# The second step of a graph layer: logits in two pairs, and one scaling moved from GpSimd to VectorE

## The chip, the cores and the metric

The kernel runs on one core of a Trainium2 chip. A core has five engines, each with its own queue of instructions, which they work off in order: TensorE (PE in the profile; its loads of the stationary operand are shown apart, as PEld), VectorE (DVE), ScalarE (ACT), GpSimd (POOL) and SyncE (SP), which here only starts transfers. They meet through semaphores. The metric is the time of one execution on the device, in microseconds; the number given is the median of several runs.

## The reference

3327 nodes with 256 features each (x), and a dense adjacency matrix (adj) in which few entries are not zero. The input is normalised and passed through a ReLU; call the result h. Then two steps run:

- `A = top_p_attention(Xa)`: for each node a query and a key of 64 numbers, `logits = q @ k.T` (3327 x 3327), a softmax over each row, of which only the largest entries that together make up 0.9 are kept; the rows are scaled to sum to one again.
- `Xf = R @ Xf` with R = adj + identity, rows scaled to sum to one, and `Xa = A @ Xa`.
- `Z = Z + Xf @ U1[n].T + Xa @ U2[n].T`.

At the end `h + Z` is normalised over the features (mean and variance), multiplied by `ln_g`, `ln_b` is added, and so is the input x.

## The kernel before, in words

The nodes are padded to 3328 and cut into NT = 26 tiles of 128 rows. For each tile and each step the kernel computes a row block e of exponentials of the logits, 128 x 3328 in fp32, finds for each row the threshold above which 0.9 of the mass lies, sets the smaller entries to zero, and multiplies what is left with the 3328 x 256 features.

All of this is a pipeline over the tiles, written out by hand. Loop i of a step works on several tiles at once, each at another stage. A loop is cut into PARTS = 7 slots. For each slot the strings in `PLAN` (and `OPEN`, `LAST` for the first and last loops of the second step) say in which order pieces of work are emitted; each letter advances one generator to its next `yield`. Since every engine works in order, and the last lines tie the order of the text as a dependency for each engine, this order is the order in each queue. The pieces of the second step, in loop i:

- w, `weights` (L580 and the lines behind): logits and exponentials of tile i + 2. Keys of even tiles stand in the lower 64 partitions of `after`, those of odd tiles in the upper 64, and so the query is held twice. Four chunks; each has two matmuls (lower and upper half, 416 columns each, L597) into one of two PSUM buffers `pl` of two banks, and an exponential on ScalarE that reads both halves (L601) with a sum. The last chunk leaves out the padded column, and a further exponential of one column (L609) makes up for it. So e has all even tiles first and then all odd ones.
- m and, in the next loop, n, `measured_twice`: estimates of the threshold of tile i + 1. It begins in `guessed`, where ScalarE adds up the partial sums in `za` to Z (L619) and goes on with small instructions (L620 to L624). Then follow three passes over e on ScalarE (L632, output `ja`), one for each of three slots, with small instructions on VectorE (L682, L683, L694, L695, L701, L702) and GpSimd (L673 to L675, L686 to L689, L703 to L707) between them.
- d and, in the next loop, c, `settle`: on VectorE the entries below the estimate (L724), the largest of each piece of 168 columns (L729) and of those again (L736, L738), sums (L743), the exact threshold, and in the first slot of the next loop the cut of e at it (L758).
- the transposes: `turn` (L804) transposes e on TensorE, four 128 x 128 blocks at a time, and ScalarE copies them to SBUF (L806). In the second step it is called at the head of each slot, before the letters; in the slot with k = 2 two groups of four are turned, and they are the first of a new tile. They need L758 of that tile to have ended.
- the sums: `sum` (L818) multiplies the transposed blocks with the features and accumulates in PSUM (`pa`), at the end of a slot. The block with number c of e belongs to feature tile `c % HALF * 2 + c // HALF`.
- s and g, `spread` and `fetching`: the product with R from gathered rows (L928 on TensorE, L1156 on VectorE; the gathers are issued by GpSimd, L920).
- f, `finish`, in four parts: the scaled sum on VectorE (L979), mean and variance on VectorE (L463, L464), the inverse deviation rstd on GpSimd (L470, L471), and in the third slot of the next loop four instructions on GpSimd: centring and scaling (L998), times gamma (L999), input plus beta (L1000), and their sum (L1001); then the row block is written out. The last tile of all does this on VectorE.

After the second step a check in the kernel proves that every threshold is exact; if it fails, a second algorithm (`search_graph_layer`) computes everything again. The first tiles of the second step have their logits computed at the end of the first one.

Of the kernel before, what the change touches and what calls it, by code (L numbers as in the profile page):

```python
# [9 lines left out]
F32 = mybir.dt.float32  # L10
# [3 lines left out]
AF = mybir.ActivationFunctionType  # L14
ALU = mybir.AluOpType
AX = mybir.AxisListType
PSUM = bass.MemoryType.PSUM

P = 128
# [3 lines left out]
NT = (N + P - 1) // P  # L23
# [301 lines left out]
HALF = NT // 2  # L325
PARTS = -(-NT // 4)
AHEAD = (2, 2)
COUNTED = [t for t in range(NT - 2) if t % 2 == 0]
HALVES = 7
FIRST = 8 * P  # L330
CUT = 4

# [12 lines left out]
def guess_graph_layer(ctx, tc, x, adj, w1t, w2t, w3t, u1t, u2t, ln_g, ln_b, out, flag):  # L347
# [10 lines left out]
    ps_l = ctx.enter_context(tc.tile_pool(name="ps_l", bufs=2, space=PSUM))  # L358
# [4 lines left out]
    V, G, S, PE = nc.vector, nc.gpsimd, nc.scalar, nc.tensor  # L363
# [10 lines left out]
    both = nodes.tile([P, 2, HALF, P], F32, tag="both", name="both")  # L374
    after = nodes.tile([P, HALF, P], F32, tag="after", name="after")
    low, high = slice(0, DA), slice(DA, P)
    keys_of = lambda step, a: after[(low, high)[a]] if step else both[(low, high)[a], a]
    query_at = lambda t: (high, low)[t % 2]
    query_of = lambda t: both[query_at(t), t % 2, t // 2, :]
    es = [nodes.tile([P, NP], F32, tag=f"e{k}", name=f"e{k}") for k in range(4)]  # L380
# [195 lines left out]
    def law_of(t):  # L576

        return lambda k: law[:, {7: 1, 8: 4}.get(k, k), t : t + 1]

    def weights(step, t, live, known=True):  # L580

        r = dict(Z=rec[:, step, 3, t : t + 1])
        qT = asked(t)
        yield
        r["ms"] = law_of(t) if known and step else early.get(t)
        lawful = law_once(step, t) if known and not step else none
        r["e"] = e = es[(2, 3, 0, 1, 4, 5)[t % 6] if step else t % 4]
        r["za"] = za = small.tile([P, CUT + 1], F32, tag="za", name="za")
        live[step, t] = r
        w = HALF * P  # L590
        wd = w // CUT
        for n in range(CUT):
            c = n * wd
            pl = ps_l.tile([P, 2, 512], F32, tag="pl", name="pl")
            for a in range(2):
                p = slice(a * DA, (a + 1) * DA)
                PE.matmul(pl[:, a, :wd], qT[p, :],  # L597
                          keys_of(step, a).rearrange("p a b -> p (a b)")[:, c : c + wd],
                          start=True, stop=True)
            if n < CUT - 1:  # L600
                S.activation(e.rearrange("p (a n) -> p a n", a=2)[:, :, c : c + wd], pl[:, :, :wd],  # L601
                             AF.Exp, accum_out=za[:, n : n + 1])
                if known and not step and n < 2:
                    r["ms"] = returned(lawful) if n else next(lawful)
                yield
            else:
                S.activation(e.rearrange("p (a n) -> p a n", a=2)[:, :, c : w - 1], pl[:, :, : wd - 1],
                             AF.Exp, accum_out=za[:, n : n + 1])
                S.activation(e[:, w - 1 : w], pl[:, 0, wd - 1 : wd], AF.Exp, accum_out=za[:, n + 1 :])  # L609
# [5 lines left out]
    def guessed(r, g, step):  # L615

        r["col"] = col = lambda k: g[:, k : k + 1]
        ms = r["ms"]
        S.activation(r["za"], r["za"], AF.Copy, accum_out=r["Z"])  # L619
        S.activation(col(0), r["Z"], AF.Ln)  # L620
        S.activation(col(2), col(0), AF.Relu, scale=-0.25, bias=ms(7))
        S.activation(col(2), col(2), AF.Exp, scale=-1.0, bias=con((6, 9)[step]))
        S.activation(col(3), col(2), AF.Square, bias=con((3, 8)[step]))
        S.activation(col(9), col(3), AF.Exp, scale=ms(3), bias=ms(8))  # L624
        return col
# [165 lines left out]
    class Sums:  # L791
# [18 lines left out]
        def sum(self, g):  # L810

            t, k = divmod(g, PARTS)
            if k == 0:
                self.pa = ps_a.tile([P, 2 * D], F32, tag="pa", name="pa")[:, :D]
            eT = self.eT.pop(g)
            for c in range(4 * k, min(4 * k + 4, NT)):
                j = c % HALF * 2 + c // HALF
                PE.matmul(self.pa, eT[:, c - 4 * k, :], self.xa[:, j, :], start=c == 0, stop=c == NT - 1)  # L818
            if k < PARTS - 1:
                return None  # L820
            if self.step:
                return t, (self.pa, self.live.pop((self.step, t))["ra"])
            n = rows_of(t)
            dst = row.tile([P, D], F32, tag="xa", name="xa", bufs=2)
            if n < P:
                V.memset(dst, 0.0)
            S.activation(dst[:n], self.pa[:n], AF.Copy, scale=self.live.pop((self.step, t))["ra"][:n])
            return t, dst
# [149 lines left out]
    def finish(t, y, pa, ra):  # L978
        V.scalar_tensor_tensor(y, pa, ra, y, ALU.mult, ALU.add)  # L979
        yield  # L980
        mv = spread_of(y)
        yield
        if t < NT - 1:
            xr = row.tile([P, D], F32, tag="xr", name="xr", bufs=1)
            nc.sync.dma_start(xr, x[t * P : (t + 1) * P])
        if t == NT - 1:
            rstd = small.tile([P, 1], F32, tag="rstd", name="rstd")
            S.activation(rstd, mv[:, 1:2], AF.Ln, bias=con(10))
            S.activation(rstd, rstd, AF.Exp, scale=-0.5)
        else:  # L990
            rstd = inverse(mv)
        yield
        if t == NT - 1:
            xr = live["x"]
            V.scalar_tensor_tensor(y, y, mv[:, 0:1], gam, ALU.subtract, ALU.mult)
            V.scalar_tensor_tensor(y, y, rstd, xr, ALU.mult, ALU.add)
        else:
            G.tensor_scalar(y, y, mv[:, 0:1], rstd, ALU.subtract, ALU.mult)  # L998
            G.tensor_tensor(y, y, gam, ALU.mult)  # L999
            G.tensor_tensor(xr, xr, bet, ALU.add)  # L1000
            G.tensor_tensor(y, y, xr, ALU.add)  # L1001
        h = rows_of(t)
        whole = h // 16 * 16
        nc.sync.dma_start(out[t * P : t * P + whole], y[:whole])
        if whole < h:
            nc.scalar.dma_start(out[t * P + whole : t * P + h], y[whole:h])
# [156 lines left out]
    def refetch(t):  # L1163
# [7 lines left out]


    PLAN = (("gmdsssaz", "gmcdsssaz", "edawwpg", "gmsdga", "gmspdea", "ohgdawwqg", "gehmgq"),
            ("llcmss", "lnms", "lwwnfd", "lcmdsssgggg", "fdswmqdf", "llmd", "lwmfdg"))

    LAST = {NT - 1: ("cfss", "cn", "nd", "sss", "fddddddsf", "f", ""), NT: ("c", "", "", "ff", "ff", "fv", "f"),
            NT + 1: ("fv", "f", "", "", "f", "f", "f")}
# [2 lines left out]
             1: ("ggmdsssbb", "gmcdgsssbb", "gedbwwbp", "bmsdg", "gmpdeg", "hgdwwqg", "hgemgqo"),  # L1180
             NT + 1: ("", "weweee", "", "", "", "", ""),
             2: ("gmdsssa", "gmcdsssga", "gedawwpg", "gmsdga", "gmspdea", "ohgdawwqg", "gehmgq")}
    OPEN = {-1: ("mxx", "mxll", "mlgg", "mgll", "mw", "mll", "mgggg"),
            0: ("cmggg", "nm", "nfd", "cmd", "fdlxmgqdf", "mwdf", "mwd"),
            1: ("cmss", "nms", "wwnfd", "cmdsssgggg", "fdsmwqdf", "mgdf", "mwdg")}
    OPEN[2] = OPEN[3] = OPEN[1]
    spacing = itertools.chain(spaced((0, 1)), *(spaced((t,)) for t in range(2, NT)))
    fetching = itertools.chain(*(refetch(t) for t in range(NT)))
# [22 lines left out]
    for step in range(2):  # L1211
        sums = Sums(step, live, xw if step else x0, AHEAD[step])

        for i in range(-1, NT + 2):
# [44 lines left out]
            for k in range(PARTS):  # L1259
# [7 lines left out]
                    prove(0)  # L1267
                g = PARTS * (i - 1) + k - LATE[step]
                summing = valid(g // PARTS)
                if step and valid((g + AHEAD[1]) // PARTS):  # L1270
                    sums.turn(g + (k == 2), min(i, NT - 1))
                for c in ({**OPEN, **LAST} if step else BEGIN).get(i, PLAN[step])[k]:
                    at = len(trace)
                    next(work[c], None)
                    if c == "g" and not step and len(trace) > at:
# [76 lines left out]
```

## Time and profile before

| what | value |
|---|---|
| median of three runs | 1305.98 us (1303.44 to 1306.17) |
| the profiled execution | 1309.6 us |
| its span, from the first to the last instruction | 1307.5 us |
| mean granted TensorE clock | 0.984 |
| busy: PE, DVE, ACT, POOL | 96%, 87%, 82%, 76% of the span |
| DMA, mean over the span | 117 GB/s |

The first step takes somewhat more than half of the span; the logits of the second one begin at 667 us, its steady part lies between some 770 and 1230 us. Busy time is the union of the instructions of an engine; matmuls overlap, and a busy PE is not PE at its peak. In the chain of waits each row names the instruction that the end waited for at that time; in a timeline the bracket says how long the engine stood idle just before and what ended it. "issue" is a wait with no cause in the profile. Times in rows are counted from the start of the span.

### The profile page before, as it was taken

The page shows a single profiled execution, that of the slowest core. Times are in us where ns is not written, and L with a number is a line of the kernel's source. Part 1 is how long each engine was busy: PE and PEld are TensorE (multiplying, and loading weights), DVE is VectorE, ACT ScalarE, POOL GpSimd, SP SyncE. Part 2 cuts the span into 40 slices and gives each one's busy share as a digit, 9 for nine tenths or more (in the row PEclk, how much of TensorE's full clock was granted, in tenths as well). Part 3 has the DMA queues.
Part 4 walks back from the last instruction along what each step waited for, and adds up shares of the span by engine and source line. Part 5 has one row for each costly group of instructions (what it writes and reads, how often), then busy time and mean ns, then how long its engine had stood idle before and what let it go on. Part 6 is the DMA issues. An engine that isn't in the chain of part 4 may idle for free.

```text
span 1307.5 us, 21855 instructions
## 1 busy us (share of the span) xinstructions
PE 1255.1 (96%) x6336; PEld 957.6 (73%) x6336; DVE 1136.7 (87%) x3437; ACT 1072.5 (82%) x2297; POOL 990.9 (76%) x1329
## 2 busy tenths in 40 slices
PE   6989899999999999999999789999999999999997
PEld 5635687777877778777777557777777777777776
DVE  6867699999999999999994579899998999999995
ACT  5375788888888888888874779999999999999961
POOL 6114788888888888888785477888888889888872
PEclk9999899999999999999999889999999999999999
DMA  8734455555455555555533231313222231322300
GB/s 289 228 124 127 146 142 150 157 147 159 138 154 153 149 158 141 145 158 151 153 88 99 76 94 51 102 55 98 72 84 81 71 98 55 98 75 79 93 22 22
DMA packets 100751, 153.11 MB, mean 117 GB/s; under 512 B 16879, under 2 KB 67182, under 8 KB 100622
## 3 DMA queue, kind: packets, MB, share of 16 engines
q1 hardware_dynamic: 83056, 108.71, 26.5%
q0 software_dynamic: 16640, 42.69, 13.0%
q8 instruction: 52, 0.85, 0.3%
q14 instruction: 77, 0.63, 0.2%
q10 hardware_dynamic: 926, 0.23, 0.1%
HBM read 120.88 MB, written 27.28 MB: 113 GB/s over the span
## 4 chain that ended last, share of the span: by engine, by line
PE 79%; DVE 7%; ACT 7%; POOL 3%; issue 2%; DMA 1%; SPq 0%; ACTq 0%; DVEq 0%; POOLq 0%
PE pa L818 38%; PE pl L597 12%; PE pt L804 10%; PE pr L928 8%; ACT ja L632 3%; PE pz L968 3%; PE pz L1044 3%; DVE cand L729 2%; PE pk L1090 1%; PE pk L490 1%; DVE x L758 1%; DVE w L724 1%; DVE cand L738 1%; DVE bb L736 1%; PE pt L479 1%
## 5 line engine op out<-in xcount | busy, mean ns | idle before, releaser
L632 ACT ACTIVATE ja<-e,g 128x3328 uint8<-128x3328 f32 x106 | 325.5, 3071 | 0.2
L818 PE MATMUL pa<-xw,eT 128*128 128x256 f32 x1352 | 322.3, 383 | 2.5 <-DVE s L979 2.5
L818 PE MATMUL pa<-x,eT 128*128 128x256 f32 x1352 | 322.6, 380 | 0.1
L818 PEld LDWEIGHTS pa<-xw,eT 128*128 128x128 f32 x1352 | 249.9, 190 | 61.8 <-issue 26.9
L818 PEld LDWEIGHTS pa<-x,eT 128*128 128x128 f32 x1352 | 243.4, 191 | 26.1 <-issue 0.4
L729 DVE MAX8 cand<-w 128x8 f32<-128x168 f32 (+1 forms) x1040 | 253.4, 319 | 0.0
L899 POOL DMA_INDIRECT ac<-in_adj,index x130 | 195.6, 1504 | 61.4 <-issue 28.0
L806 ACT COPY eT<-pt 128x512 f32<-128x512 f32 (+1 forms) x364 | 198.3, 552 | 49.5 <-PE pt L804 44.2
L920 POOL DMA_INDIRECT xg<-vx,index x130 | 191.3, 1471 | 34.7 <-issue 33.0
L920 POOL DMA_INDIRECT xg<-bx,index x130 | 157.2, 1209 | 48.5 <-issue 23.8
L804 PEld LDWEIGHTS pt<-ident,e 128*128 128x128 f32 x1144 | 138.9, 143 | 58.5 <-issue 30.5
L804 PE MATMUL pt<-ident,e 128*128 128x128 f32 x1144 | 176.5, 277 | 3.0 <-ACT mq L531 1.3
L724 DVE SCALAR_TENSOR_TENSOR w<-e,g 128x3328 f32<-128x3328 f32 x44 | 162.3, 3688 | 0.9
L928 PE MATMUL pr<-xg,ac 128*128 128x257 f32 (+1 forms) x520 | 139.3, 392 | 9.7 <-DVE s L1156 5.7
L758 DVE SCALAR_TENSOR_TENSOR e<-e,rec 128x3328 f32<-128x3328 f32 x40 | 147.2, 3680 | 0.6
L601 ACT ACTIVATE e<-pl 128x832 f32<-128x832 f32 x132 | 114.2, 867 | 37.7 <-PE pl L597 29.6
L928 PEld LDWEIGHTS pr<-xg,ac 128*128 128x128 f32 x520 | 94.1, 193 | 36.7 <-issue 14.4
L597 PE MATMUL pl<-both,qT 64*128 64x416 f32 x416 | 97.8, 548 | 7.1 <-DVE e L1050 3.6
L597 PE MATMUL pl<-after,qT 64*128 64x416 f32 x416 | 96.2, 556 | 0.1
L848 DVE TENSOR_REDUCE fm<-at 128x4 f32<-128x512 f32 (+1 forms) x133 | 84.5, 636 | 0.0
L736 DVE MAX8 bb<-cand 128x8 f32<-128x160 f32 x234 | 75.6, 323 | 4.6
L632 ACT ACTIVATE ja<-x,g 128x3328 uint8<-128x3328 f32 x24 | 73.6, 3065 | 0.0
(270 smaller groups left out, 1995.4 us busy)
## 6 DMA issues: line engine op xcount, KB each, us to landing
at<-in_adj SPq DMA_DIRECT2D x114, 256.0 KB
cx<-ac SPq DMA_DIRECT2D x26, 384.0 KB
ac<-cx SPq DMA_DIRECT2D x26, 384.0 KB
wide<-in_adj SPq DMA_DIRECT2D x8, 832.0 KB
e<-in_adj SPq DMA_DIRECT2D x6, 832.0 KB
own<-bx SPq DMA_DIRECT2D x26, 128.5 KB
x<-in_x SPq DMA_DIRECT2D x13, 256.0 KB
qT<-both SPq DMA_DIRECT2D x104, 32.0 KB
```

What stands on the lines that cost most here:

```text
L597: PE.matmul(pl[:, a, :wd], qT[p, :], keys_of(step, a).rearrange("p a b -> p (a b)")[:, c : c + wd], start=True, stop=True)
L601: S.activation(e.rearrange("p (a n) -> p a n", a=2)[:, :, c : c + wd], pl[:, :, :wd], AF.Exp, accum_out=za[:, n : n + 1])
L632: S.activation(ja, e, f, bias=guess, scale=sign, accum_out=total)
L724: V.scalar_tensor_tensor(w, e, col(16), e, ALU.is_lt, ALU.mult, accum_out=d2)
L729: V.max(cand[:, 8 * s : 8 * s + 8], w[:, s * SEG : min(NP, (s + 1) * SEG)])
L758: V.scalar_tensor_tensor(e, e, at(1), e, ALU.is_ge, ALU.mult, accum_out=ra)
L804: PE.transpose(pt[:, j, :], e[:, (j0 + j) * P : (j0 + j + 1) * P], ident)
L806: S.copy(eT[:, :w, :], pt[:, :w, :])
L818: PE.matmul(self.pa, eT[:, c - 4 * k, :], self.xa[:, j, :], start=c == 0, stop=c == NT - 1)
L899: G.indirect_dma_start(out=ac[:, k, :], out_offset=None, in_=rows, in_offset=bass.IndirectOffsetOnAxis(ap=index[:, t, k : k + 1], axis=0), ...
L920: G.indirect_dma_start(out=xg[:, k, :w], out_offset=None, in_=rows, in_offset=bass.IndirectOffsetOnAxis(ap=index[:, t, k : k + 1], axis=0))
L928: PE.matmul(pr[:, :w], ac[:, k, :], own if k == KT - 1 else xg[:, k, :w], start=k == 0, stop=k == KT - 1)
```

## The change

All parts but the tables of order concern the second step alone.

- The four chunks of logits are cut at tile pairs: 4, 3, 3 and 3 pairs, so 512, 384, 384 and 384 columns in each half (`EDGES`). Each chunk is written to e as a block of its own, even tiles and then odd ones, and `ORDER` says which feature tile a block of e belongs to. For the last chunk the lower half is written at the end of its PSUM bank, so that both halves follow each other without a gap and one exponential of 767 columns leaves out the padded column. The exponential of one column is gone.
- Z is summed on VectorE (a reduction of four numbers) in a fifth call of w, and no longer in `guessed`.
- The letters w: two in slot k = 2, one in k = 4 and one in k = 6 become two in k = 2, two in k = 4 and the fifth call in k = 6.
- A letter t places the transposes inside a slot. In k = 2 they now come behind the two w; where a slot has no t they stay at its head.
- In `finish`, L998 goes from GpSimd to VectorE for all tiles but the last.

```diff
+EDGES = (0, 4, 7, 10, 13)
+ORDER = ([2 * j + h for h in range(2) for j in range(HALF)],
+         [2 * j + h for a, b in zip(EDGES, EDGES[1:]) for h in range(2) for j in range(a, b)])
...
+    def close(qT, e, za):
+
+        keys = after.rearrange("p j r -> p (j r)")
+        for n, (j0, j1) in enumerate(zip(EDGES, EDGES[1:])):
+            c, w = j0 * P, (j1 - j0) * P
+            pl = ps_l.tile([P, 2, 512], F32, tag="pl", name="pl")
+            for p, at in ((low, pl[:, 0, 512 - w :] if n == CUT - 1 else pl[:, 0, :w]), (high, pl[:, 1, :w])):
+                PE.matmul(at, qT[p, :], keys[p, c : c + w], start=True, stop=True)
+            to = e[:, 2 * c : 2 * (c + w)]
+            if n == CUT - 1:
+                S.activation(to[:, : 2 * w - 1], pl.rearrange("p a n -> p (a n)")[:, 512 - w : 511 + w], AF.Exp,
+                             accum_out=za[:, n : n + 1])
+            else:
+                S.activation(to.rearrange("p (a n) -> p a n", a=2), pl[:, :, :w], AF.Exp, accum_out=za[:, n : n + 1])
+            yield
...
+        if step:
+            yield from close(qT, e, za)
+            V.tensor_reduce(r["Z"], za[:, :CUT], AX.X, ALU.add)
+            return
...
-        S.activation(r["za"], r["za"], AF.Copy, accum_out=r["Z"])
+        if step == 0:
+            S.activation(r["za"], r["za"], AF.Copy, accum_out=r["Z"])
...
-                j = c % HALF * 2 + c // HALF
-                PE.matmul(self.pa, eT[:, c - 4 * k, :], self.xa[:, j, :], start=c == 0, stop=c == NT - 1)
+                PE.matmul(self.pa, eT[:, c - 4 * k, :], self.xa[:, ORDER[self.step][c], :], start=c == 0, stop=c == NT - 1)
...
-            G.tensor_scalar(y, y, mv[:, 0:1], rstd, ALU.subtract, ALU.mult)
+            V.tensor_scalar(y, y, mv[:, 0:1], rstd, ALU.subtract, ALU.mult)
...
-            ("llcmss", "lnms", "lwwnfd", "lcmdsssgggg", "fdswmqdf", "llmd", "lwmfdg"))
+            ("llcmss", "lnms", "wwtlnfd", "lcmdsssgggg", "fdswwmqdf", "llmd", "lwmfdg"))
...
-    OPEN = {-1: ("mxx", "mxll", "mlgg", "mgll", "mw", "mll", "mgggg"),
+    OPEN = {-1: ("mxx", "mxll", "mlgg", "mgll", "mw", "mllw", "mgggg"),
...
-            1: ("cmss", "nms", "wwnfd", "cmdsssgggg", "fdsmwqdf", "mgdf", "mwdg")}
+            1: ("cmss", "nms", "wwtnfd", "cmdsssgggg", "fdsmwwqdf", "mgdf", "mwdg")}
...
-                if step and valid((g + AHEAD[1]) // PARTS):
-                    sums.turn(g + (k == 2), min(i, NT - 1))
-                for c in ({**OPEN, **LAST} if step else BEGIN).get(i, PLAN[step])[k]:
+                plan = ({**OPEN, **LAST} if step else BEGIN).get(i, PLAN[step])[k]
+                for c in plan if "t" in plan or not step else "t" + plan:
+                    if c == "t":
+                        if valid((g + AHEAD[1]) // PARTS):
+                            sums.turn(g + (k == 2), min(i, NT - 1))
+                        continue
```

More of the change, by code (lines that the diff above doesn't have):

```diff
@@ L376, in guess_graph_layer @@
     low, high = slice(0, DA), slice(DA, P)
-    keys_of = lambda step, a: after[(low, high)[a]] if step else both[(low, high)[a], a]
+    keys_of = lambda a: both[(low, high)[a], a]
     query_at = lambda t: (high, low)[t % 2]
@@ L597, in weights @@
                 PE.matmul(pl[:, a, :wd], qT[p, :],
-                          keys_of(step, a).rearrange("p a b -> p (a b)")[:, c : c + wd],
+                          keys_of(a).rearrange("p a b -> p (a b)")[:, c : c + wd],
                           start=True, stop=True)
@@ L602, in weights @@
                              AF.Exp, accum_out=za[:, n : n + 1])
-                if known and not step and n < 2:
+                if known and n < 2:
                     r["ms"] = returned(lawful) if n else next(lawful)
```

## The prediction

> **What bounds the kernel now.** I read the page first (busy time, then the chain that ended last), then the busy time of the middle of the second step, then the chain there in order of time, and last the instructions of one tile engine by engine.
>
> ```profile
> PE 1255.1 (96%) x6336; PEld 957.6 (73%) x6336; DVE 1136.7 (87%) x3437; ACT 1072.5 (82%) x2297; POOL 990.9 (76%) x1329
> ...
> PE 79%; DVE 7%; ACT 7%; POOL 3%; issue 2%; DMA 1%; SPq 0%; ACTq 0%; DVEq 0%; POOLq 0%
> ```
>
> ```profile
> 860.00:1230.00 370.00, 369.05 (x1895) 286.99 (x1896) 342.10 (x1002) 355.47 (x681) 322.08 (x412) 1.00 0.27 80
> ```
>
> The second row is busy time between 860 and 1230 us in the order PE, PEld, DVE, ACT, POOL, then granted clock (1.00). PE is never idle, but ACT stands at 96%, DVE at 92% and POOL at 87%: a gain on PE is soon stopped by another engine, so all four are counted. One tile on the chain (start, length, count of instructions):
>
> ```profile
> 900.79 0.44 PE pt L804 x4
> 901.23 0.90 PE pl L597 x4
> 902.12 1.92 PE pa L818 x8
> ...
> 904.49 1.73 PE pa L818 x8
> ...
> 906.65 0.90 PE pl L597 x4
> ...
> 917.48 1.60 PE pl L597 x8
> 919.08 1.49 PE pr L928 x6
> ...
> 921.44 0.44 PE pt L804 x4
> ```
>
> From turn to turn, 900.79 to 921.44, a tile takes 20.65 us, and PE sets it. The logits (pl) come in three groups, x4, x4 and x8. Twice 0.90 against 1.60 says that 0.70 us is the work of four instructions and 0.20 us a fixed cost of each group. What follows a group is dear too: 1.92 against 1.73 us for the same eight sums, and 1.49 us against 6 x 0.216 = 1.30 for the six pr. So entering and leaving the logits costs 0.20 + 0.19 = 0.39 us a group, 1.17 a tile.
>
> **The change, part by part.** *Logits on PE.* Four chunks of 416 columns become 512 + 384 + 384 + 384; that is 1664 columns in both cases, and at 0.70 us per 416 the work stays 2.80 us. I take the time as linear in the columns. Three groups become two, so PE loses one fixed cost: 20.65 - 0.39 = 20.26 us a tile. By the code the pattern stands in 23 tiles, and from the first to the last of these rows PE is the chain:
>
> ```profile
> 855.54 1.60 PE pl L597 x8
> ...
> 1228.35 1.60 PE pl L597 x8
> ```
>
> 372.81 us are 18 periods of 20.65 and 1.1 us of stall, so 19 tiles are counted in full: 19 x 0.39 = 7.4 us. Four tiles lie before 855.
>
> *Exponentials on ACT.* The same elements are read, in four instructions. The one-column exponential (L609) and the copy that sums (L619) go; what they take is from their start to the next start:
>
> ```profile
> 905.11 3.07 ACT L632 ACTIVATE ja<-e,g 128x3328 uint8<-128x3328 f32 x1
> ...
> 908.64 0.87 ACT L607 ACTIVATE e<-pl 128x830 f32<-128x830 f32 x1
> ...
> 909.48 0.17 ACT L609 ACTIVATE e<-pl 128x1 f32<-128x1 f32 x1
> ...
> 909.63 0.39 ACT L697 ACTIVATE g<-g,one 128x1 f32<-128x1 f32 x1
> ...
> 911.06 0.20 ACT L619 ACTIVATE za<-za 128x5 f32<-128x5 f32 x1
> ...
> 911.38 0.20 ACT L620 ACTIVATE g<-rec 128x1 f32<-128x1 f32 x1
> ```
>
> 0.15 + 0.32 = 0.47 us. ACT's work a tile is 355.47 / 370 x 20.65 = 19.84, after it 19.37, under 20.26.
>
> *Work put on DVE.* A sum of four numbers (L733 is the nearest row) and the centring and scaling of a 128x256 row block, which leaves POOL.
>
> ```profile
> 906.26 0.15 DVE L733 TENSOR_REDUCE rec<-cand 128x1 f32<-128x20 f32 x1
> 906.33 0.32 DVE L736 MAX8 bb<-cand 128x8 f32<-128x160 f32 x1
> ...
> 908.56 0.27 DVE L694 TENSOR_SCALAR g<-oa,g 128x1 f32<-128x1 f32 x1
> ...
> 911.55 0.58 POOL L471 TENSOR_TENSOR rstd<-rstd,half 128x1 f32<-128x1 f32 x1
> ...
> 911.64 3.69 DVE L758 SCALAR_TENSOR_TENSOR e<-e,rec 128x3328 f32<-128x3328 f32 x1
> ...
> 912.32 4.00 POOL L920 DMA_INDIRECT xg<-vx,index  x1 [0.19 <-issue]
> ...
> 915.45 3.66 DVE L724 SCALAR_TENSOR_TENSOR w<-e,g 128x3328 f32<-128x3328 f32 x1
> ...
> 916.23 1.01 PEld L804 LDWEIGHTS pt<-ident,e 128*128 128x128 f32 x8
> ...
> 916.38 2.95 POOL L673 TENSOR_SCALAR g<-g,law 128x1 f32<-128x1 f32 x1
> ...
> 920.03 1.25 POOL L998 TENSOR_SCALAR s<-s,mv,rstd 128x256 f32<-128x256 f32 x1
> ...
> 921.37 0.73 POOL L999 TENSOR_TENSOR s<-s,gam 128x256 f32<-128x256 f32 x1
> ...
> 921.48 0.48 DVE L979 SCALAR_TENSOR_TENSOR s<-pa,ra,s 128x256 f32<-128x256 f32 x1 [0.83 <-PE pa L818]
> ```
>
> ```profile
> L878 DVE TENSOR_SCALAR oh<-place,over,lists 128x128 f32<-128x128 f32 x26 | 9.0, 345 | 0.8 <-ACT lists L874 0.8
> ...
> L746 DVE TENSOR_SCALAR dr<-cum,need 128x40 f32<-128x40 f32 x26 | 6.5, 249 | 0.9
> ```
>
> An instruction that does not need the one ahead starts 0.08 us before that one ends (906.26 + 0.15 against 906.33). So the sum of four adds 0.07. For the 256 columns I extend the two TENSOR_SCALAR rows: (345 - 249) / 88 = 1.09 ns a column, 345 + 128 x 1.09 = 485 ns, 0.40 net of the overlap; below it lies the 128-column row (0.26 net), above it 0.485 + 0.15 with no overlap at all. DVE's only wait in the tile is 0.83 us at L979, with the lost overlap 0.91: its work is 19.74 us, after it 20.21 (20.07 to 20.38). Against PE's 20.26 that is a dead heat with 0.05 us left. At the upper end DVE sets 20.38, which costs 0.12 x 19 = 2.3 us; I take 0.4.
>
> *Logits ahead of the new tile's transposes.* These transposes need L758, which ends at 915.33; they begin at 916.23, 0.90 us of room. With a pair of logits ahead (512 + 384 columns: 1.5 us, and 0.2 to enter) the room becomes 2.6. It is needed: both exponentials of the second pair now stand ahead of the count (ja, 905.11 + 3.07 = 908.18) whose result L694 waits for. That count ends some 0.8 us later relative to PE (0.87 x 768 / 832); L694 at 908.56 has under 0.4 us of room, so DVE slides back by about 0.5 us, and the room at the transposes stays above 2. The next tile's sums must not start before L979 has read PSUM; ahead of them stands a pair of 1.5 us where one chunk of 0.9 stood, so a later L979 is covered too.
>
> *POOL.* Without L998 each tile has 921.37 - 920.03 = 1.34 us less. L999 now waits for DVE, where the new instruction stands between L758 and L724; POOL is then still inside L673, so it is not late. The new wait is DVE's for rstd (L471), with L724 and the whole search for the tile's threshold queued behind it. Today L471 starts 0.09 us before L758 and is done (912.13) 3.2 us before L758 ends: hidden. Uncovered, it is the slower rival.
>
> *Ends.* Before 855 the chain runs through other engines, with this POOL instruction held while DVE runs L758:
>
> ```profile
> 828.54 3.61 POOL g L705
> ```
>
> The waits between engines from 760 us on (total, times, longest) show what PE lost to late transposes, and a wait of DVE with no cause that the profile shows:
>
> ```profile
> DVE g L694 <- issue: 3.6, 6, 2.0
> ...
> PE pt L804 <- DVE x L758: 1.8, 2, 1.0
> ```
>
> The four early tiles gain 0 (the same holds recur) to 2.4 us (4 x 0.39, and 0.8, the smaller of the two late transposes, which the new room of 2.6 us would cover); I take 1.2. Of the 1.1 us of stall behind 855, which lies at the other late transpose, I take 0.5 back: its cause, DVE's 2.0 us, stays.
>
> After the last logits DVE is the chain:
>
> ```profile
> 1243.10 3.70 DVE x L758 x2
> ...
> 1267.08 3.62 DVE w L724 x2
> ```
>
> Here the moved instruction is on the path, twice: 2 x 0.40, and DVE arrives there up to 0.9 us later against PE (0.5 slid, 0.4 from the dead heat): a loss of 0 to 1.7, I take 1.2.
>
> Sum: 7.4 + 1.2 + 0.5 - 1.2 - 0.4 = 7.5 us. The profiled execution took 1309.6 us (span 1307.5), 3.6 above the median of 1305.98; its own time becomes 1302.1, and in the terms of the median 1298.5. Bounds of the terms: 7.4 - 1.7 - 2.3 = 3.4, and 7.4 + 2.4 + 1.1 = 10.9, so 1295.1 to 1302.6.
>
> **The rivals.** *DVE takes over.* If L694 keeps waiting 0.3 us in each tile for the later count, DVE needs 20.5: 19 x 0.15 + 0.5 - 1.2 = 2.2 us, 1303.8. For it: 0.05 us is no margin. Against it: DVE can slide back by two us before PE waits.
>
> *Pairs wait for ACT.* If a pair's second chunk finds its PSUM buffer unread, the fixed cost is spent again inside the pair: no gain on PE, the tail's 1.2 lost, stalls 0.5 back, about 1306.7. Against it: the pairs start 4.4 us apart at the closest (901.23 + 20.65 - 917.48), and the two exponentials of 0.87 each follow the first pair at once.
>
> *Slower: DVE waits for rstd.* If POOL starts L471 behind L758, it is held until L758 ends, as L705 was (3.61 us); L673 ended 0.2 us after L724 did, then 0.58 for L471: the new instruction stalls 0.75 us, DVE needs 20.96, PE's gain is gone and 0.31 a tile is lost: 23 x 0.31 + 1.2 = 8.3 us, 1314.3. The point: from L724's end (919.11) POOL needs 13.09 us to its next L471 (911.55 + 20.65), then 11.75; DVE comes to L758 in 13.18, then 13.18 - 0.91 + 0.07 = 12.34. So POOL must lose 0.59 us in every tile. Margin today 0.09, so the removal of L998 speaks against it; a POOL delay also sends DVE back, which restores the margin in the next tile.
>
> *Slower: the gather in flight.* L920 runs to 916.32, 0.99 us past L758's end. If a running gather kept DVE from the moved instruction, DVE would need 21.20: 23 x 0.55 + 1.2 = 13.9 us, 1319.9. The nearest rows show an instruction of this kind inside a gather at its usual length:
>
> ```profile
> 343.54 1.11 POOL L899 DMA_INDIRECT ac<-in_adj,index  x1 [0.19 <-issue]
> 343.95 0.34 DVE L878 TENSOR_SCALAR oh<-place,over,lists 128x128 f32<-128x128 f32 x1
> ```
>
> The Trainium skill has this as a rule ("SBUF — State Buffer", section "SBUF: two separate sides"): VectorE and GpSimd share a port pair; of two instructions that need it, whichever starts first holds it to its end and the other fully blocks. By that rule this rival would be the forecast; the trace agrees for POOL behind L758 (4.00 us) but not for L878 behind a gather (0.34 us).
>
> *The kernel doesn't do what it says.* The columns of e stand in another order, so another spread of large entries over the 168-column pieces is searched; if the proof fails, the second algorithm runs and the time more than doubles.
>
> **How the numbers follow.** The forecast (1298.5) 0.60, DVE takes over 0.17, pairs wait 0.08, rstd 0.10, gather 0.03, proof 0.02. About 0.2%, 2.6 us, is what a measurement can tell from no change: faster means under 1303.4, slower over 1308.6. Faster: 0.60 and half of DVE's 0.17, 0.68. Same: the other half and the pairs, 0.17. Slower 0.15. The range 1294 to 1307 holds the forecast's own and the two rivals without change; the slower 0.15 is left out, with little below.
>
> **What would show it.** Right: logits in x8 groups only, 1.7 and 1.5 us; a tile of 20.2 to 20.3 us on the chain; L979 nearly without wait; L998 on DVE in 0.4 to 0.5 us; transposes never waiting for L758. Wrong: a wait of DVE at L998 for L471 (slower), a wait at L694 in every tile (DVE takes over), PE idle between two chunks of a pair (ACT), or fixed costs that stay with each pair of chunks rather than with each group.

## The result, and the profile after

The changed kernel takes 1298.88 us (median; 1293.95 to 1301.80) against 1305.81 (1300.52 to 1308.65) for the kernel before, timed in the same rounds: a ratio of 0.9948, 95% interval 0.9935 to 0.9961, or 5.1 to 8.5 us less. 1298.5 had been forecast.

Busy time and the chain that ended last, from the page after:

```profile
PE 1237.1 (96%) x6336; PEld 950.1 (73%) x6336; DVE 1146.6 (89%) x3488; ACT 1060.7 (82%) x2193; POOL 975.3 (75%) x1304
...
PE 47%; DVE 42%; ACT 5%; issue 3%; POOL 2%; DMA 1%; SPq 0%; ACTq 0%; POOLq 0%; DVEq 0%
```

PE held 79% of the chain and DVE 7%; now they share it. The busy times of the middle of the second step after (columns as before: PE, PEld, DVE, ACT, POOL, clock) say the same:

```profile
860.00:1215.00 355.00, 353.70 (x1854) 280.19 (x1853) 341.26 (x1002) 339.11 (x600) 308.90 (x383) 1.00 0.26 80
```

DVE went from 92% to 96%, ACT stays at 96%, POOL stays at 87% of a shorter tile, and PE at over 99%.

The spans of the two profiled executions (1307.5 and 1294.2 us) differ by more than the change gives: the first step, whose work is unchanged, was some 8 us shorter in the second of them, and over the profiles of this study its end scatters by 11 us. So the second step is compared alone. Its tiles are counted by the threshold cut on DVE (L758 before, L782 after). The first and the last of the 24 cuts, before:

```profile
787.24 3.69 DVE L758 SCALAR_TENSOR_TENSOR e<-e,rec 128x3328 f32<-128x3328 f32 x1
...
1262.77 3.69 DVE L758 SCALAR_TENSOR_TENSOR e<-e,rec 128x3328 f32<-128x3328 f32 x1
```

and after:

```profile
780.47 3.69 DVE L782 SCALAR_TENSOR_TENSOR e<-e,rec 128x3328 f32<-128x3328 f32 x1
...
1247.81 3.69 DVE L782 SCALAR_TENSOR_TENSOR e<-e,rec 128x3328 f32<-128x3328 f32 x1
```

23 tiles took 475.5 us and take 467.3: 8.2 us less. Behind the last cut the end came 44.7 us later and now comes 46.3 later, 1.6 us lost; from the step's first logarithm to the first cut it was 59.9 and is 61.2, but that stretch lies anywhere between 59.9 and 61.7 in the profiles of this study.

The chain of waits after, in order of time (start, length, instruction), runs through DVE for tiles on end:

```profile
842.50 3.71 DVE x L782 x2
...
846.40 0.31 DVE s L1021
846.71 3.61 DVE w L748 x2
...
862.60 3.71 DVE x L782 x2
...
882.66 3.71 DVE e L782 x2
...
886.56 0.54 DVE s L1021
...
902.95 3.71 DVE e L782 x2
```

From cut to cut it is 20.10, 20.06 and 20.29 us. The tile with 20.29 is the one in which the moved scaling (L1021) adds 0.54 us to the chain where it adds 0.31 in the others. One tile later on takes 21.96 us (the hold: time that is lost in the same tile of every kernel here, see the last section); over the tiles of 20.0 to 20.3 us the mean is 20.17. And the logits stand in pairs only; PE's instructions after:

```profile
906.24 1.77 PE L590 MATMUL pl<-after,qT 64*128 64x512 f32 x8
907.94 1.09 PE L828 MATMUL pt<-ident,e 128*128 128x128 f32 x8
...
911.56 1.56 PE L590 MATMUL pl<-after,qT 64*128 64x384 f32 x8
...
926.44 1.77 PE L590 MATMUL pl<-after,qT 64*128 64x512 f32 x8
```

From the first pair of one tile to that of the next it is 20.20 us. In all but three of the 18 tiles from 845 to 1211 us it is 20.21, and between 860 and 1215 us PE is idle for 1.3 us in all (355.00 less 353.70 in the row of busy times), at the hold alone. So PE still sets the pace of the steady part, and DVE, in tiles of 20.06 and 20.28 us, has as good as no room beside it; the chain can be led through either.

The waits between engines after, from 760 us on (total, times, longest), show no wait that comes back in every tile of DVE:

```profile
PE pa L841 <- DVE s L1002: 7.4, 6, 2.3
DVE s L1002 <- PE pa L841: 6.3, 1, 6.3
...
PE pt L828 <- DVE e L782: 1.0, 1, 1.0
PE pt L828 <- DVE x L782: 1.0, 2, 0.5
...
DVE s L1021 <- POOL rstd L474: 0.3, 1, 0.3
```

DVE's wait for the sums (L979 before, 0.83 us in each tile) is now one wait, at the very end (L1002, 6.3 once). The transposes wait for the cut three times, once at the hold and twice behind the last logits. The feared wait for rstd came once.

### The profile page after: what moved, and what is told of

The parts are those of the page before. It is cut to its first block, busy times and chain, and to the rows that moved or that the text cites. A ratio compares the mean times of both kernels' runs of the same rounds, so it can differ in the third digit from the quotient of the medians.

```text
span 1294.2 us, 21775 instructions
## 1 busy us (share of the span) xinstructions
PE 1237.1 (96%) x6336; PEld 950.1 (73%) x6336; DVE 1146.6 (89%) x3488; ACT 1060.7 (82%) x2193; POOL 975.3 (75%) x1304
## 4 chain that ended last, share of the span: by engine, by line
PE 47%; DVE 42%; ACT 5%; issue 3%; POOL 2%; DMA 1%; SPq 0%; ACTq 0%; POOLq 0%; DVEq 0%
PE pa L841 20%; DVE cand L753 9%; DVE w L748 8%; PE pl L620 6%; PE pt L828 5%; DVE e L782 5%; PE pr L951 4%; DVE cand L762 3%; DVE bb L760 3%; PE pz L1067 3%; PE pz L991 3%; ACT ja L656 2%; DVE x L782 2%; PE pl L590 1%; PE pk L1113 1%
## 5 line engine op out<-in xcount | busy, mean ns | idle before, releaser
L922 POOL DMA_INDIRECT ac<-in_adj,index x130 | 184.5, 1420 | 60.5 <-issue 27.8
L943 POOL DMA_INDIRECT xg<-vx,index x130 | 200.2, 1540 | 34.7 <-issue 32.8
L943 POOL DMA_INDIRECT xg<-bx,index x130 | 167.5, 1288 | 48.1 <-issue 24.7
L748 DVE SCALAR_TENSOR_TENSOR w<-e,g 128x3328 f32<-128x3328 f32 x44 | 163.0, 3705 | 0.9
L782 DVE SCALAR_TENSOR_TENSOR e<-e,rec 128x3328 f32<-128x3328 f32 x40 | 147.2, 3681 | 0.6
L951 PE MATMUL pr<-xg,ac 128*128 128x257 f32 (+1 forms) x520 | 135.3, 384 | 9.4 <-DVE s L1179 5.8
L590 PE MATMUL pl<-after,qT 64*128 64x384 f32 (+1 forms) x416 | 90.7, 548 | 0.0
L624 ACT ACTIVATE e<-pl 128x832 f32<-128x832 f32 x78 | 67.7, 868 | 25.8 <-PE pl L620 23.1
L697 POOL TENSOR_SCALAR g<-g,law 128x1 f32<-128x1 f32 x23 | 76.9, 3344 | 3.4 <-ACT g L696 2.3
```

The source lines that it names most:

```text
L748: V.scalar_tensor_tensor(w, e, col(16), e, ALU.is_lt, ALU.mult, accum_out=d2)
L782: V.scalar_tensor_tensor(e, e, at(1), e, ALU.is_ge, ALU.mult, accum_out=ra)
L922: G.indirect_dma_start(out=ac[:, k, :], out_offset=None, in_=rows, in_offset=bass.IndirectOffsetOnAxis(ap=index[:, t, k : k + 1], axis=0), ...
L943: G.indirect_dma_start(out=xg[:, k, :w], out_offset=None, in_=rows, in_offset=bass.IndirectOffsetOnAxis(ap=index[:, t, k : k + 1], axis=0))
L951: PE.matmul(pr[:, :w], ac[:, k, :], own if k == KT - 1 else xg[:, k, :w], start=k == 0, stop=k == KT - 1)
```

## The experiments

All ratios are against the kernel before, run on the same chip in the same rounds. "23 tiles" is the time from the first to the last cut, "tile" the median distance of two cuts (without holds: of the tiles of 20.0 to 20.3 us), both from the one profiled execution of each kernel.

| kernel | ratio, 95% interval | 23 tiles, us | tile, us |
|---|---|---|---|
| before | 1 | 475.5 | 20.64 |
| after | 0.9948 (0.9935 to 0.9961) | 467.3 | 20.27 (mean without holds 20.17) |
| after_again (after, repeated) | 0.9930 (0.9911 to 0.9950) | 466.9 | 20.15 (mean without holds 20.14) |
| y_pool | 1.0002 (0.9980 to 1.0025) | 474.5 | 20.31 |
| three_groups | 0.9979 (0.9962 to 0.9996) | 471.9 | 20.60 |
| turn_first | 1.0001 (0.9984 to 1.0018) | 473.6 | 20.48 |
| more_dve | 1.0005 (0.9990 to 1.0020) | 473.3 | 20.47 |
| only_y | 0.9998 (0.9978 to 1.0019) | 473.4 | 20.64 |
| order_only | 0.9983 (0.9968 to 0.9999) | 473.5 | 20.31 |
| pairs_y | 0.9976 (0.9958 to 0.9994) | 470.4 | 20.31 |
| y_act | 1.0213 (1.0184 to 1.0242) | 502.4 | 21.90 |
| y_act2 | 0.9972 (0.9954 to 0.9989) | 471.0 | 20.31 |
| y_behind | 0.9940 (0.9922 to 0.9958) | 466.2 | 20.20 |

### One part undone

**y_pool**: the scaling back on GpSimd, all else as after.

```
-            V.tensor_scalar(y, y, mv[:, 0:1], rstd, ALU.subtract, ALU.mult)
+            G.tensor_scalar(y, y, mv[:, 0:1], rstd, ALU.subtract, ALU.mult)
```

> The changed kernel with centring and scaling (L1021) back on GpSimd; all else stays. My theory: in the changed kernel VectorE sets a tile at 20.06 to 20.28 us, TensorE's own work is 20.20. Without L1021 VectorE needs 0.31 to 0.54 less, TensorE sets 20.20, so the middle stays as it is, the sums' wait for L1002 goes, and the end gains up to 1 us: 1297 to 1300. Rival A, the move off GpSimd made the gain: GpSimd is 1.3 us later in each tile, L718 waits for L710, back to 1303 to 1306.

The gain in the time is gone (of the 8.2 us in the 23 tiles 1.0 is left): rival A, and not the theory. PE and DVE both have less to do than 20.31 us here, so neither sets the tile. POOL and DVE around the third count's first reader (L718), from the instructions in order of time:

```profile
898.00 2.96 POOL L697 TENSOR_SCALAR g<-g,law 128x1 f32<-128x1 f32 x1
...
901.66 1.25 POOL L1021 TENSOR_SCALAR s<-s,mv,rstd 128x256 f32<-128x256 f32 x1
...
905.37 1.04 POOL L943 DMA_INDIRECT xg<-vx,index  x1 [0.16 <-issue]
...
910.24 0.26 POOL L710 TENSOR_SCALAR g<-g 128x1 f32<-128x1 f32 x1
...
910.54 0.27 DVE L718 TENSOR_SCALAR g<-oa,g 128x1 f32<-128x1 f32 x1 [0.48 <-POOL g L710]
...
918.31 2.95 POOL L697 TENSOR_SCALAR g<-g,law 128x1 f32<-128x1 f32 x1
```

From L697, which is held until DVE's L748 ends, POOL goes on through the scaling, the rest of the row block and the gathers to L710 with no gap over 0.30 us; L718 starts 0.04 us behind L710's end; behind L718 come the rest of the search, the cut and the next L748, which again holds L697. From L697 to L697 it is 20.31 us: a round through two engines, neither of which is full. The scaling's 1.25 us is a link of it. On DVE it costs 0.31 to 0.54 us; on POOL it set the tile.

**three_groups**: the second pair undone; the third and the fourth chunk of a tile stand apart again, each now 384 columns wide.

```
-            ("llcmss", "lnms", "wwtlnfd", "lcmdsssgggg", "fdswwmqdf", "llmd", "lwmfdg"))
+            ("llcmss", "lnms", "wwtlnfd", "lcmdsssgggg", "fdswmqdf", "llmd", "lwmfdgw"))
...
-            1: ("cmss", "nms", "wwtnfd", "cmdsssgggg", "fdsmwwqdf", "mgdf", "mwdg")}
+            1: ("cmss", "nms", "wwtnfd", "cmdsssgggg", "fdsmwqdf", "mgdf", "mwdgw")}
```

> The changed kernel with the third and fourth chunk of logits apart again (two, one, one); the sum of Z stays on VectorE, at the end of the slot. My theory: a group costs TensorE a fixed 0.39 us, so a tile takes 20.6 us in 20 tiles and all but 1 us of the gain goes: 1304 to 1307. Rival B, the gain is ScalarE's shorter work and the room ahead of the transposes: no more than 1 us is lost, 1298 to 1300.

The time (1300.50 us, beside 1303.91 for the kernel before) lies lower than the theory had it. The chain through PE:

```profile
1052.87 0.86 PE pa L841 x4
...
1054.17 0.85 PE pl L590 x4
...
1059.54 0.84 PE pl L590 x4
...
1069.45 1.70 PE pl L590 x8
...
1073.47 0.86 PE pa L841 x4
```

From x4 to x4 a tile of PE takes 20.60 us. The kernel y_behind below shows PE's own tile with two groups, 20.20. One group costs 0.40 us, as forecast (0.39), and PE sets the tile. But of the 8.2 us in the 23 tiles 3.6 are left: DVE has some 0.4 us of room in such a tile, and makes good what the hold costs it. PE's 18 tiles from 843 to 1214 us are all of 20.60, without a stall. The three early tiles are shorter, too (20.38, 20.37 and 20.15 us; the kernel after has 20.85, 21.13 and 20.06); the same room may be the reason, but this was not followed.

**turn_first**: the new tile's transposes ahead of the first pair again.

```
-            ("llcmss", "lnms", "wwtlnfd", "lcmdsssgggg", "fdswwmqdf", "llmd", "lwmfdg"))
+            ("llcmss", "lnms", "wwlnfd", "lcmdsssgggg", "fdswwmqdf", "llmd", "lwmfdg"))
...
-            1: ("cmss", "nms", "wwtnfd", "cmdsssgggg", "fdsmwwqdf", "mgdf", "mwdg")}
+            1: ("cmss", "nms", "wwnfd", "cmdsssgggg", "fdsmwwqdf", "mgdf", "mwdg")}
```

> The changed kernel with the new tile's transposes in front of the first pair of logits, as before. My theory: the cut of e ends some 0.4 us behind the point where TensorE comes to the pair, so the transposes wait, but VectorE sets the tile, and its own round does not lead over these transposes: 0 to 2 us slower than the changed kernel, 1299 to 1301. Rival C, the new room is what the gain is: 1303 to 1306, with a wait of the transposes for the cut in each tile.

I expected a small loss, and the gain in the time went (of the 8.2 us in the 23 tiles 1.9 are left): rival C. DVE and PE's weight loads around the cut:

```profile
1093.76 3.68 DVE L782 SCALAR_TENSOR_TENSOR x<-x,rec 128x3328 f32<-128x3328 f32 x1
1097.37 0.08 DVE L782 DVE_READ_ACCUMULATOR x<-x,rec 128x1 f32 x1
...
1097.57 0.86 PEld L828 LDWEIGHTS pt<-ident,x 128*128 128x128 f32 x8 [0.41 <-issue]
```

and the waits between 860 and 1215 us:

```profile
ACT e L596 <- PE pl L590: 4.9, 11, 0.5
DVE g L718 <- ACT ja L656: 2.8, 9, 0.3
```

The transposes' weights start 0.12 us behind the cut; the pair follows them; ACT waits for the pair; the exponentials push ACT's counts back; L718 waits for the last count; and behind L718 comes the next cut. That round takes 20.48 us. A pair ahead of the transposes does more than fill a gap: the exponentials then no longer depend on the cut, and the round is open.

**more_dve**: one more instruction on DVE per tile, a statistic of 0.41 us that nobody reads.

```
+        if t < NT - 1:
+            V.bn_stats(small.tile([P, 6], F32, tag="bn", name="st2"), y)
```

> The changed kernel with a second, unused bn_stats of 128x256 on VectorE in each tile but the last (0.41 us, 0.33 net of the overlap). My theory, VectorE sets the tile: 22 to 25 tiles x 0.33 = 7 to 8 us slower than the changed kernel, 1305 to 1308, with longer waits of the sums for L1002. If TensorE set the tile and VectorE had the room: under 1 us, 1299 to 1300.

Its tiles take 20.38 or 20.60 us where after has 20.06 or 20.28, so it adds 0.32 us to DVE's tile. The 23 tiles grow by 6.0 us, 0.26 each: all but 0.06 us of it shows. DVE has next to no room; the dead heat of the forecast is real, and the time is as the theory had it (1305.13 us).

### One part alone

**only_y**: the kernel before, with the scaling on DVE. **order_only**: the kernel before, with the new order alone (two pairs, the first ahead of the transposes, by the letter t), chunks of 416 columns and the scaling on GpSimd. **pairs_y**: both, still with the one-column exponential (L609) and ScalarE's sum (L619).

```
 only_y, pairs_y:
-            G.tensor_scalar(y, y, mv[:, 0:1], rstd, ALU.subtract, ALU.mult)
+            V.tensor_scalar(y, y, mv[:, 0:1], rstd, ALU.subtract, ALU.mult)
 order_only, pairs_y:
-            ("llcmss", "lnms", "lwwnfd", "lcmdsssgggg", "fdswmqdf", "llmd", "lwmfdg"))
+            ("llcmss", "lnms", "wwtlnfd", "lcmdsssgggg", "fdswwmqdf", "llmd", "lmfdg"))
...
-            1: ("cmss", "nms", "wwnfd", "cmdsssgggg", "fdsmwqdf", "mgdf", "mwdg")}
+            1: ("cmss", "nms", "wwtnfd", "cmdsssgggg", "fdsmwwqdf", "mgdf", "mdg")}
```

> The kernel before with the scaling on VectorE alone. My theory: three groups keep TensorE at 20.65 us a tile, so the middle stays; VectorE at 20.2 wins back less after a hold, GpSimd's round is shorter, the end loses up to 0.8: 1304 to 1307, no difference. Rival, the move alone is the gain: 1299 to 1302.

> The kernel before with the order of logits and transposes alone (pairs, the first ahead of the transposes); old chunks, scaling on GpSimd. My theory: TensorE could do 20.2 us a tile, but the round of GpSimd and VectorE over L686 and L694 sets 20.3, and each hold is kept in full: 1302 to 1306, as with the scaling put back on GpSimd. Rival, the order is the gain by itself: 1298 to 1301.

> The kernel before with two parts of the change: logits in pairs with the first pair ahead of the transposes, and the scaling on VectorE. The four chunks of 416 columns, the one-column exponential and ScalarE's sum of Z stay. My theory: groups and rounds are those of the changed kernel, ScalarE has 0.47 us more a tile but is not the bound: 20.2 to 20.3 us a tile, 1298 to 1301. Rival, ScalarE's shorter work is a needed part: 20.5 or more, 1303 to 1306.

only_y keeps PE's 20.64 and gains only in the early tiles and at the hold; order_only stops at 20.31, where L694 waits for GpSimd in every tile, the same round as in y_pool. Both times are as forecast. The waits of order_only between 860 and 1215 us:

```profile
DVE g L694 <- POOL g L686: 12.4, 18, 3.0
```

pairs_y stops at 20.30 too, though GpSimd no longer has the scaling. The instructions around L694 there:

```profile
1126.35 3.07 ACT L632 ACTIVATE ja<-e,g 128x3328 uint8<-128x3328 f32 x1
...
1128.33 0.26 POOL L686 TENSOR_SCALAR g<-g 128x1 f32<-128x1 f32 x1
...
1129.32 0.19 ACT L632 ACTIVATION_READ_ACCUMULATOR ja<-e,g 128x1 f32 x1
...
1129.62 0.27 DVE L694 TENSOR_SCALAR g<-oa,g 128x1 f32<-128x1 f32 x1 [0.22 <-POOL g L689]
...
1130.18 0.39 ACT L697 ACTIVATE g<-g,one 128x1 f32<-128x1 f32 x1 [0.19 <-DVE g L695]
```

The view names POOL L689, whose result L694 does not read; L686, which it reads, had ended 1.03 us earlier. The count's sum ended at 1129.51, 0.11 us before L694, and this 0.11 returns wherever L694 or L718 waits for ACT (0.04 where it waits for GpSimd). So it is ACT's round: count, L694 and L695 on DVE, L697, and on through ACT's tile with no gap over 0.09 us to the next count, 20.30 us for 19.76 us of work. In order_only this round is close behind GpSimd's: there the count ends 0.11 to 0.14 us ahead of L694, but at the hold. The time forecast for pairs_y came (1300.94 us), but not the reason: ACT is the bound, as the rival had it, at a smaller size. Only the 0.47 us that the change takes off ACT brings this round under the others. Its length in the kernel after, 20.30 - 0.47 = 19.83 us, is worked out; no run shows it by itself.

So the parts do not add up. Alone the scaling saves 2.1 us of the 23 tiles and the order 2.0; both save 5.1; with the folded column and sum and the wider chunks it is 8.2. These are single profiles; the two of the kernel after differ by 0.5 us.

### The scaling in other places

**y_act**: the scaling on ScalarE, its bias formed by a small GpSimd operation just ahead of it.

```
-            V.tensor_scalar(y, y, mv[:, 0:1], rstd, ALU.subtract, ALU.mult)
+            G.tensor_scalar(mv[:, 0:1], mv[:, 0:1], rstd, -1.0, ALU.mult, ALU.mult)
+            S.activation(y, y, AF.Identity, scale=rstd, bias=mv[:, 0:1])
```

> The changed kernel with centring and scaling on ScalarE: one activation of 128x256 with rstd as scale and minus mean times rstd as bias, the bias made by one small instruction on GpSimd. My theory, as the first four runs leave it: in a tile TensorE needs 20.2 us, VectorE 20.1 to 20.3, the round of GpSimd and VectorE over L710 and L718 20.3 with the scaling on GpSimd and 19.0 without. With it on ScalarE, VectorE needs 19.8, GpSimd's round 19.3, ScalarE under 20: TensorE alone sets 20.2, and VectorE can win back 0.4 us a tile after each hold. 0 to 3 us faster than the changed kernel, 1296 to 1299. Rival: ScalarE's later counts hold L718, 20.4 or more a tile, 1301 to 1304.

It loses 2.1%, which neither the theory nor the rival had. The waits between 860 and 1215 us:

```profile
ACT s L1022 <- POOL mv L1021: 26.4, 17, 1.6
DVE g L706 <- ACT ja L656: 22.1, 16, 1.4
```

The 0.27 us operation stands on POOL behind L697, which is held to the end of DVE's L748. ACT, in order, waits 1.55 us a tile for it, its count comes late, and DVE waits for the count.

**y_act2**: the same, but the bias formed right behind L474, before the gather.

```
             rstd = inverse(mv)
+            G.tensor_scalar(mv[:, 0:1], mv[:, 0:1], rstd, -1.0, ALU.mult, ALU.mult)
...
-            V.tensor_scalar(y, y, mv[:, 0:1], rstd, ALU.subtract, ALU.mult)
+            S.activation(y, y, AF.Identity, scale=rstd, bias=mv[:, 0:1])
```

> The kernel after with the scaling of the row block on ScalarE, as in the earlier trial, but the bias (minus mean times rstd) is formed by GpSimd right behind L474, half a tile before ScalarE needs it, so that it is not held behind VectorE's L748. Theory: the loss of that trial (1.55 us a tile) was this wait alone. VectorE loses 0.31 to 0.54 us (19.75 a tile), ScalarE gains some 0.45 (19.3 to 19.8), GpSimd 0.27; TensorE's 20.20 sets the tile, and VectorE has 0.4 us of room to win back what a hold costs: 1295 to 1298.5. Rival: ScalarE's 19.8 is packed around its dependencies, so that 0.45 us more in front of a count makes VectorE wait for it at L706 or L718: tile 20.4 to 20.7, 1302 to 1308. Second rival: GpSimd's extra instruction delays its gather behind L782 and so everything behind it by 0.3 us a tile: waits of VectorE for GpSimd at L718, 1301 to 1304.

That wait is gone, and the tile is 20.31 us, not 20.2: the first rival, with a smaller size. The instructions around the cut:

```profile
1114.61 3.32 POOL L1015 TENSOR_SCALAR mv<-mv,rstd 128x1 f32<-128x1 f32 x1
...
1121.23 0.61 ACT L1022 ACTIVATE s<-s,mv,rstd 128x256 f32<-128x256 f32 x1
...
1131.06 0.19 ACT L656 ACTIVATION_READ_ACCUMULATOR ja<-e,g 128x1 f32 x1
...
1131.36 0.27 DVE L718 TENSOR_SCALAR g<-oa,g 128x1 f32<-128x1 f32 x1 [0.46 <-issue]
```

The small operation is still held (3.32 us, now by the cut), which costs nothing here. The scaling adds 0.51 us to ACT (to the next start), about as much as L609 and L619 had, and L718 again starts 0.11 us behind the count: ACT's round, at the length it had in pairs_y. The chunks here are those of the kernel after, so their widths are not what made that round long.

**y_behind**: the scaling on DVE behind L748 instead of ahead of it; no other compute instruction changes its place.

```
-            ("llcmss", "lnms", "wwtlnfd", "lcmdsssgggg", "fdswwmqdf", "llmd", "lwmfdg"))
+            ("llcmss", "lnms", "wwtlndf", "lcmdsssgggg", "fdswwmqdf", "llmd", "lwmfdg"))
...
-            1: ("cmss", "nms", "wwtnfd", "cmdsssgggg", "fdsmwwqdf", "mgdf", "mwdg")}
+            1: ("cmss", "nms", "wwtndf", "cmdsssgggg", "fdsmwwqdf", "mgdf", "mwdg")}
```

> The kernel after with one instruction moved: the scaling of the row block (0.40 us in some tiles, 0.62 in the others) stands on VectorE behind L748 instead of in front of it. Nothing else changes. Theory G (the gather in flight lengthens it): in front of L748 the instruction overlaps the end of a gather in about half the tiles; behind L748 no gather runs, so it takes 0.40 us in every tile, VectorE's tile is a uniform 20.06, TensorE's 20.20 sets the period, and the time falls by 0 to 3 us against the kernel after: 1296 to 1299. Rival B (the two durations belong to the row buffers or the instruction itself): 0.40 and 0.62 alternate as before, tile 20.17, 1298 to 1300. Rival W (GpSimd now waits for it, or it meets GpSimd's small instructions there): the gathers of the next tile and L710 come later, L718 waits, tile over 20.3, 1301 to 1304.

The moved instruction's durations (minimum, median, maximum in ns), in the kernel after:

```profile
L1021 DVE TENSOR_SCALAR s<-s,mv,rstd x25: 394/412/625, 805.1 to 1276.4; 128x256 f32<-128x256 f32 x25
```

and in y_behind:

```profile
L1021 DVE TENSOR_SCALAR s<-s,mv,rstd x25: 395/405/412, 814.0 to 1280.3; 128x256 f32<-128x256 f32 x25
```

Behind L748 none of 25 is lengthened. In the seven profiles that have the scaling on DVE ahead of L748, 39 of the 141 scalings that start inside a gather take 0.62 us, and none of the other 34. So the 0.62 us belongs to this place, where a gather is in flight, and not to a row buffer; why it comes in some tiles only is open. The time is that of the kernel after (1300.23 us, beside 1299.25 for after_again). With VectorE at 20.05, the late tiles stand at 20.20 one behind the other: that is PE's own tile, which no gain on VectorE can pass. So theory G holds, at the lower end of the gain that it gave.

> The kernel after, unchanged, beside the two others on one chip: 1297 to 1300, tile alternating between 20.06 and 20.28 us on VectorE.

It repeats the result (1299.25 us), but with 3 scalings of 25 at 0.62 us, where the first profile has 11. The time does not notice, since PE's 20.20 stands next to it.

## Why the prediction held, point by point

**PE's groups: right.** 0.39 us a group had been read from the chain; 0.40 was measured (20.60 with three, 20.20 with two). The Trainium skill ("TensorEngine Tiling (Array Packing)", section "Key Properties") says that changing the tiling mode drains TensorE; the fixed 0.40 us of each group of 64-row logits between 128-row work fits this, but no trace shows what it consists of. PE's tile came to 20.20, not 20.26: the kernel three_groups, at 20.60 against the 20.65 before, shows 0.05 us that has nothing to do with the groups. The new chunk widths, which had been taken as free of effect, are one possible reason; no run separates them.

**DVE's dead heat: right.** 20.21 (20.07 to 20.38) had been forecast, 20.05 to 20.28 came, mean 20.17. The scaling takes 0.39 to 0.41 us in most tiles and 0.62 in some; 0.485 had been extended from rows of another width, too steeply.

**The gains, term by term.** The prediction counted on PE, from the row at 855.54 us to that at 1228.35: 372.81 us, which are 18 tiles of 20.65 and 1.1 us of stall. The same two rows after:

```profile
845.61 1.77 PE L590 MATMUL pl<-after,qT 64*128 64x512 f32 x8
...
1210.87 1.77 PE L590 MATMUL pl<-after,qT 64*128 64x512 f32 x8
```

They are 365.26 us apart: 18 tiles of 20.21, 1.4 us of stall at the hold, and 0.1 in two tiles of 20.25 and 20.28. So the large term was not too large: PE gained 0.44 us a tile, where 0.39 had been counted, and of the 0.4 set aside for DVE no more than that 0.1 shows. The term that was wrong in sign is the 0.5 us taken back of the stall, which grew by 0.3. In sum these 18 tiles gained 7.55 us, where 7.1 had been counted (18 x 0.39 + 0.5 - 0.4). The four tiles ahead of them gained 0.6 (83.8 to 83.2 us; forecast 1.2). Counted at DVE's cuts, the same gain is 1.35 in the three early tiles (63.39 to 62.04), 0.8 in the tile of the hold (22.78 to 21.96) and 6.0 in the other 19: before, DVE won back part of the hold in tiles of 20.31 us; after, it has no room for that. The 8.2 us less the 1.6 lost at the end are 6.6 (the start of the step, which scatters by 1.8 us, is left out), beside 6.9 between the two medians and 7.5 in the forecast. That the total came so close is in part luck: terms missed by up to 0.9 us, in both directions.

**The tail: right in kind.** 1.2 us of loss forecast, 1.6 measured; in all profiles with the scaling on GpSimd the end comes 44.7 to 45.1 us behind the last cut, with it on DVE or ACT 45.6 to 46.4.

**ACT: the step failed, without harm.** "ACT's work a tile is 19.84, after it 19.37, under 20.26", and so the 0.47 us was costed at nothing. pairs_y shows that the engine's round, with the waits in it, was 20.30 and would have been the bound. Busy time was compared where the length of a round was wanted.

**POOL: the same error.** "Without L998 each tile has 1.34 us less" was costed at nothing. y_pool shows that without this part the gain in the time is gone. That L673 ended only behind L724, and that the rest of POOL's tile stands behind it, was in the rows; the round was not followed to its end.

**The room at the transposes: right, but too small.** It was costed as cover for 0.5 to 0.8 us of lateness. turn_first shows a round of 20.48 us that this order opens; without it there is no gain in the time.

**The rivals.** No wait of DVE at L694 (now L718) in each tile, none of ACT between two chunks, and one for rstd, of 0.3 us. The gather in flight lengthened the scaling by 0.23 us in 11 of 25 tiles of one profile and in 3 of another, far from the 0.99 us of the rival. The rule that the prediction drew on (the Trainium skill, "SBUF — State Buffer", section "SBUF: two separate sides") is one for two instructions that need the shared port pair: the later one fully blocks. That the scaling needs the pair had been assumed, and no run shows it blocked until the gather ends. In one tile after, by the instructions in order of time, the scaling starts and ends inside a gather and takes 0.40 us:

```profile
903.09 4.54 POOL L943 DMA_INDIRECT xg<-vx,index  x1 [0.19 <-issue]
...
906.76 0.40 DVE L1021 TENSOR_SCALAR s<-s,mv,rstd 128x256 f32<-128x256 f32 x1
```

GpSimd's small operations behind a long two-input instruction of VectorE do agree (L1015, 3.32 us).

So the time was right, and the sum had the right large term; that three other rounds (20.31, 20.30 and 20.48 us with one part missing) lay within about 0.3 us of the new tile, and that the parts taken as harmless were each needed, the forecast did not see. That all three came out under PE's tile was luck as far as the forecast goes.

## What to carry to other kernels

When several engines stand near 90%, a tile is set by rounds through two or three engines as much as by one engine's work; follow what holds the first link of a queue until the chain returns to the same instruction one tile later, and compare those lengths, not busy times. A release can be told by its lag: here 0.11 us behind ScalarE's count and 0.04 behind GpSimd, whatever engine a view names. Judge a change with several parts by undoing each: here less than half of the 8.2 us in the 23 tiles was left with the pairs, the order or the scaling undone, and 5.1 with the work put back on ScalarE and the old chunks.

## What the runs showed of the hardware

A one-column GpSimd operation of 0.27 us can take 3.3 us when VectorE is inside a two-input instruction of 3328 columns; where another engine reads its result, the place of such an operation decides. In y_act the operation stands behind another that is held so, and ScalarE waits 1.55 us for it in each tile; in y_act2 it is held itself, and that costs nothing.

VectorE's scaling of 128x256 takes 0.39 to 0.41 us, or up to 0.63 with a gather in flight. The gather is in flight in nearly every tile and the number of lengthened ones changes from one execution of the same kernel to the next, so what decides it stays open.

In one tile, the same in all 13 profiles, a GpSimd gather starts 2.6 us late, and the cut there comes 0.6 to 2.5 us later than in the other tiles (the hold spoken of above). It is in the waits of the kernel after, between 860 and 1215 us:

```profile
POOL xg L943 <- issue: 23.5, 82, 2.6
```

In other runs the view names a transpose on PE for this wait. What holds the gather was not found, and no run here removed it; in three_groups PE does not wait there.
